# The first image's 5x5 convolution computed by pairs of rows with shared products

## The chip, the core and the metric

The kernel runs on one core of one Trainium2 chip. The metric is the device time in microseconds of one execution. A core has five engines that run side by side, each with its own queue of instructions in order: TensorE (PE, matrix products into PSUM), VectorE (DVE), ScalarE (ACT), GpSimd (POOL) and SyncE (SP, which here issues DMA transfers). They wait for each other by semaphores.

## What is computed

Four images of 128 channels and 64 x 64 pixels pass through four layers, each with a group normalisation ahead of it and the input added to its result. All data is float32. Cut to what matters:

```
x = x + attention(group_norm(x))        # layer 0, all 4096 pixels against all
x = x + conv5x5(group_norm(x), c)       # layer 1, 128 -> 128 channels, zero padding 2
x = x + selective_scan(group_norm(x))   # layer 2, a recurrence over the 4096 pixels
x = x + conv3x3(group_norm(x), main_w)  # layer 3, 128 -> 128 channels, zero padding 1
```

The 25 taps `c` of layer 1 are themselves built from tables (`weightsxx`, `weightsidentity`, picked by the radius of the tap), so they are computed on the chip at the start.

## The kernel before

Channels lie on the 128 partitions, pixels along the free dimension. The program is written as Python generators: `images()` strings together the work of the four images for everything except the recurrence, and `scan_core` is the recurrence itself, in ticks of 1024 pixels. Each `yield` hands back an estimate of the TensorE time just recorded (`PRODUCT`, 0.86 us for one 128x512 product). The loop at L1088 records one tick of the scan and then as much of `images()` as a credit (`pace`) allows, so the order of the instructions on every engine is written out by hand, and the work of images 1 to 3 is laid between the ticks of the scan of earlier images. Image 0 has no scan to lie beside: its attention is recorded first (L1060 to L1066, with the building of the 5x5 taps laid into its start), and then `before(0)` draws its convolution and the first part of its scan preparation before the first tick.

`conv` (L542) does a convolution. It clears the borders of a padded copy of the image, `xp` (L549 to L552, four memsets on GpSimd), normalises the image into it in four quarters on ScalarE (`piece`), and then, for each of 8 blocks of 8 rows (512 pixels), adds up k x k products in one PSUM bank:

```
nc.tensor.matmul(
    acc.rearrange("p (r w) -> p r w", w=W), weights[:, t, :],
    xp[:, y : y + RPM, dx : dx + W],
    start=t == 0, stop=t == k * k - 1 and not residual,
)
```

Each tap is one weight matrix of 128 x 128, and each product reads 8 rows of 64 pixels, shifted by the tap. Banks go round by the tags `s`, `a`, `z`. After the third product of the next block, `finish` takes the block away. For layer 1 this is `add` (L952): VectorE adds the bank to `xs`, the running image, and takes the statistics (`bn_stats`) for the next group norm. Then `scan_prep` (L590) normalises `xs` and goes on.

The names that matter below: `xs` the running image; `xp` (in traces `xpe` for layer 1, `xpm` for layer 3) the padded normalised image; `cw` the 25 taps; `m3` the 9 taps of layer 3, loaded at the start on ScalarE's queue (L111); `pce` the PSUM bank of a block; tags `A0`, `A1`, `V` and `xt` the large buffers of which each convolution takes one. `build_conv_weights` (L214) makes `cw` on VectorE. `L405`, `L411`, `L417` are the attention's scores, exponentials and values, `L459` its sums of exponentials, taken on VectorE and GpSimd for image 0. `L808` and `L839` are the GpSimd products of the scan, `L818` its recurrence on VectorE, and `br`, `cr` the rows that it loads through SyncE's queue (L784). The whole program is recorded twice; the second copy (`program(True)`), a safer form of the attention, runs only where a sum of exponentials has left its range.

Of the kernel before, what the change touches and what calls it, by code (L numbers as in the profile page):

```python
# [24 lines left out]
F32 = mybir.dt.float32  # L25
I32 = mybir.dt.int32
AF = mybir.ActivationFunctionType
ALU = mybir.AluOpType
# [4 lines left out]
P = 128  # L33
GROUPS = 32
GN_EPS = 1e-5
CH = 1024
MM = 512
HALF = P // 2
PAD = 2
# [6 lines left out]
PRODUCT, HOP, SLOT, PACE, ENDPACE, AHEAD = 0.86, 1.7, 0.7, 2.9, 1.5, 4  # L46
# [6 lines left out]
def conv_preact_kernel(  # L53
# [16 lines left out]
    nc = tc.nc  # L70
    B, C, H, W = x.shape
    L = H * W
# [4 lines left out]
    NTAP = xhat.shape[1]  # L77
    HP, WP = H + 2 * PAD, W + 2 * PAD
# [3 lines left out]
    RPM = MM // W  # L82
# [4 lines left out]
    const = ctx.enter_context(tc.tile_pool(name="const", bufs=1))  # L87
    small = ctx.enter_context(tc.tile_pool(name="small", bufs=2))
    dram = ctx.enter_context(tc.tile_pool(name="dram", bufs=2, space=DRAM))
    ps = ctx.enter_context(tc.tile_pool(name="ps", bufs=1, space=PSUM))  # L90
    pools, ready = {}, set()

    def bank(tag, name):
        return pools.get(tag, ps).tile([P, MM], F32, tag=tag, name=name)
# [12 lines left out]
    nc.scalar.dma_start(wback[:, 0, :], mats[:, 4, :])  # L107
    nc.scalar.dma_start(wback[:HALF, 1, :], mats[HALF:, 4, :])
    nc.scalar.dma_start(wback[HALF:, 1, :], mats[:HALF, 4, :])
    m3 = const.tile([P, main_w.shape[1], C], F32, name="m3")  # L110
    nc.scalar.dma_start(m3, main_w)  # L111

    ident = const.tile([P, P], F32, name="ident")
    make_identity(nc, ident)
# [18 lines left out]
    for d in range(2):  # L133
        r = slice(d * HALF, (d + 1) * HALF)
# [74 lines left out]
    nc.vector.tensor_scalar(hbias, cbias, 0.5, None, ALU.mult)  # L209


    cw = const.tile([P, NTAP, C], F32, name="cw")

    def build_conv_weights(tmp):  # L214
        xx_sb = tmp.tile([P, NTAP, C], F32, name="xx_sb")
        nc.sync.dma_start(xx_sb, xhat)
        id_sb = tmp.tile([P, C], F32, name="id_sb")
        nc.sync.dma_start(id_sb, identity)
        picked = tmp.tile([P, 2, NTAP, C // 2], F32, name="picked")
        for n, (which, table, inds) in enumerate((("xx", wxx, indsxx), ("id", wid, indsid))):  # L220
            nr, oc = table.shape[1], table.shape[2]
            acc = picked[:, n]
            one = cw.rearrange("p k c -> p (k c)")[:, : NTAP * oc]
            one = one.rearrange("p (k o) -> p k o", o=oc)
            tab = tmp.tile([P, nr, oc], F32, name=f"tab{which}")
            nc.sync.dma_start(tab, table)
            ii = tmp.tile([P, NTAP], I32, name=f"ii{which}")
            nc.sync.dma_start(ii, inds.to_broadcast([P, NTAP]))
            fi = tmp.tile([P, NTAP], F32, name=f"fi{which}")
            nc.vector.tensor_copy(fi, ii)  # L230

            ng = tmp.tile([P, NTAP], F32, name=f"ng{which}")
            nc.vector.tensor_scalar(ng, fi, 0.0, float(nr), ALU.is_lt, ALU.mult)
            nc.vector.tensor_tensor(fi, fi, ng, ALU.add)
            nc.vector.tensor_scalar(fi, fi, 0.0, float(nr - 1), ALU.max, ALU.min)
            for r in range(nr):
                hit = tmp.tile([P, NTAP], F32, name=f"hit{which}{r}")
                nc.vector.tensor_scalar(hit, fi, float(r), None, ALU.is_equal)
                hit_b = hit.unsqueeze(2).to_broadcast([P, NTAP, oc])
                tab_b = tab[:, r : r + 1, :].to_broadcast([P, NTAP, oc])  # L240
                if r == 0:
                    nc.vector.tensor_tensor(acc, tab_b, hit_b, ALU.mult)
                else:
                    nc.vector.tensor_tensor(one, tab_b, hit_b, ALU.mult)
                    nc.vector.tensor_tensor(acc, acc, one, ALU.add)
                yield HOP

        for t in range(2):
            def every(ap):
                return ap.rearrange("p k (o t) -> p k o t", t=2)[:, :, :, t]  # L250

            idb = id_sb.rearrange("p (o t) -> p o t", t=2)[:, :, t].unsqueeze(1)
            idb = idb.to_broadcast([P, NTAP, C // 2])
            nc.vector.tensor_tensor(every(xx_sb), every(xx_sb), picked[:, 0], ALU.mult)
            nc.vector.tensor_tensor(every(cw), picked[:, 1], idb, ALU.mult)
            yield HOP
        nc.vector.tensor_tensor(cw, cw, xx_sb, ALU.add)

    ASIZE, VSIZE = (H + 4) * (W + 4), (H + 2) * (W + 2)

    def large(n, name):
        return pools["big"].tile([P, ASIZE], F32, tag=f"A{n % 2}", name=name)
# [6 lines left out]
    def stats_tile(name):  # L272
        return small.tile([P, NM, 6], F32, tag=f"gn_st{name[0]}", name=f"st_{name}")
# [36 lines left out]
    def normalise(dst, src, gn):  # L310
        nc.scalar.activation(dst, src, AF.Identity, scale=gn[0], bias=gn[1])  # L311
# [230 lines left out]
    def conv(b, xs, tag, st, weights, k, finish, name, residual=False):  # L542

        pad = k // 2
        hp, wp = H + 2 * pad, W + 2 * pad
        size = VSIZE if tag == "V" else ASIZE
        xp = pools["big"].tile([P, size], F32, tag=tag, name=f"xp{name}_{b}")
        xp = xp[:, : hp * wp].rearrange("p (h w) -> p h w", w=wp)
        nc.gpsimd.memset(xp[:, :pad, :], 0.0)  # L549
        nc.gpsimd.memset(xp[:, hp - pad :, :], 0.0)  # L550
        nc.gpsimd.memset(xp[:, pad : hp - pad, :pad], 0.0)
        nc.gpsimd.memset(xp[:, pad : hp - pad, wp - pad :], 0.0)  # L552
        gn = yield from group_norm(st, f"{name}{b}")
        xh = xs.rearrange("p (h w) -> p h w", w=W)

        def piece(i):
            h0, h1 = i * H // 4, (i + 1) * H // 4
            normalise(xp[:, pad + h0 : pad + h1, pad : pad + W], xh[:, h0:h1, :], gn)

        piece(0)  # L560
        yield HOP / 2
        piece(1)
        done = None
        for i in range(NM):
            if i < 2:
                piece(2 + i)
            acc = bank("saz"[i % 3], f"pc{name}_{b}_{i}")
            for t in range(k * k):
                dy, dx = divmod(t, k)
                y = i * RPM + dy  # L570
                nc.tensor.matmul(  # L571
                    acc.rearrange("p (r w) -> p r w", w=W), weights[:, t, :],
                    xp[:, y : y + RPM, dx : dx + W],
                    start=t == 0, stop=t == k * k - 1 and not residual,
                )
                if t == 2 and done is not None:
                    finish(*done)
                if t % 3 == 2:
                    yield 3 * PRODUCT
            if residual:  # L580
                nc.tensor.matmul(acc, ident, xs[:, bass.ts(i, MM)], start=False, stop=True)
            yield PRODUCT
            done = i, acc
        yield HOP
        finish(*done)

# [334 lines left out]
    def program(safe):  # L923
        mats4, ynds, ends = {}, {}, {}
        ready.clear()

        def load(tile, b):
            for c in range(NCH):
                nc.sync.dma_start(tile[:, bass.ts(c, CH)], xf[b][:, bass.ts(c, CH)])
                yield 0.0  # L930
# [13 lines left out]
        def front(b, xn, v):  # L944

            xs = large(b + 1, f"xs_{b}")[:, :L]
            yield from load(xs, b)
            st = stats_tile(f"e{b}")
            yield from attention(b, xs, xn, v, st, safe)
            st2 = stats_tile(f"s{b}")  # L950

            def add(i, acc):  # L952
                cut = bass.ts(i, MM)
                nc.vector.tensor_tensor(xs[:, cut], acc, xs[:, cut], ALU.add)
                nc.vector.bn_stats(st2[:, i, :], xs[:, cut])

            yield from conv(b, xs, f"A{b % 2}", st, cw, 5, add, "e")

            def mat(name):
                return dram.tile([NCH, P, CH], F32, tag=name, name=f"{name}_{b}")  # L960

            mats4[b] = (
                [mat("bm"), mat("cm")], mat("dd"), mat("dxd"), mat("xcd"),
                dram.tile([P, L], F32, tag="xsd", bufs=B, name=f"xsd_{b}"),
            )
            ynds[b] = dram.tile([NM, P, MM], F32, tag="ynd", bufs=B, name=f"ynd_{b}")
            operands = yield from scan_prep(b, xs, st2, mats4[b])
            if b + 1 < B:
                return (yield from both(operands, start(b + 1, 10)))
            yield from operands  # L970
# [52 lines left out]
        inner, last = range(PER, NM - PER), range(NM - PER, NM)  # L1023
# [15 lines left out]
        with ExitStack() as es, tc.manual_schedule():  # L1039
# [60 lines left out]
            for _ in chain(end(B - 1, range(PER)), back(B - 1)):  # L1100
                pass

    program(False)


# [11 lines left out]
    with tc.If(again > 0):  # L1117
        program(True)
# [59 lines left out]
```

## Time and profile before

| | |
|---|---|
| time, median of 3 runs | 4684.2 us (4680.76 to 4685.26) |
| span of the profiled run | 4679.2 us, mean granted TensorE clock 0.941 |
| TensorE matmul | 4151.4 us busy (89%) |
| VectorE | 3764.6 us busy (80%) |
| GpSimd | 3522.0 us busy (75%) |
| ScalarE | 2313.3 us busy (49%) |
| HBM | 153 GB/s over the span |
| the convolution of image 0 (L571) | 542.3 to 717.5 us of the span, 400 records of 200 products |

Engines work side by side, so the busy times don't add up. The shares are means over stages that differ, and what an edit is worth has to be read in the stage in which it lies. A float32 product of 128x512 appears as two MATMUL records. A line such as `L571 PE MATMUL pce<-xpe,cw 128*128 128x512 f32 x400 | busy, mean ns | idle before, releaser` reads: source line, engine, operation, output and inputs, shape, count; time in which the group kept its engine busy, mean length of one; time for which the engine stood idle ahead of it, and what ended most of that.

### The profile page before, as it was taken

The page shows a single profiled execution, that of the slowest core. Times are in us where ns is not written, and L with a number is a line of the kernel's source. Part 1 is how long each engine was busy: PE and PEld are TensorE (multiplying, and loading weights), DVE is VectorE, ACT ScalarE, POOL GpSimd, SP SyncE. Part 2 cuts the span into 40 slices and gives each one's busy share as a digit, 9 for nine tenths or more (in the row PEclk, how much of TensorE's full clock was granted, in tenths as well). Part 3 has the DMA queues.
Part 4 walks back from the last instruction along what each step waited for, and adds up shares of the span by engine and source line. Part 5 has one row for each costly group of instructions (what it writes and reads, how often), then busy time and mean ns, then how long its engine had stood idle before and what let it go on. Part 6 is the DMA issues. An engine that isn't in the chain of part 4 may idle for free. (4 is left out here: it accounts for less than half of the span.)

```text
span 4679.2 us, 43928 instructions
## 1 busy us (share of the span) xinstructions
PE 4151.4 (89%) x13840; PEld 1538.3 (33%) x13840; DVE 3764.6 (80%) x3673; ACT 2313.3 (49%) x4166; POOL 3522.0 (75%) x1644
## 2 busy tenths in 40 slices
PE   6999997999999988999999979999999748576767
PEld 3444443333333323333333323333333202121212
DVE  7222104999999998999999999899989899999993
ACT  2333205666665356666654466666543644444431
POOL 2333202898888978898989869888889689999992
PEclk9999998999999999999999989999999968787878
DMA  1000005544444555445444564454445565656561
GB/s 65 0 0 1 0 5 184 186 168 163 163 169 150 178 203 214 155 164 175 169 158 164 187 227 169 157 177 164 168 147 177 201 224 199 229 193 229 186 230 46
DMA packets 210434, 718.90 MB, mean 154 GB/s; under 512 B 24848, under 2 KB 25744, under 8 KB 210064
## 3 DMA queue, kind: packets, MB, share of 16 engines
q1 hardware_dynamic: 208448, 714.69, 43.7%
q8 instruction: 111, 1.82, 0.2%
q10 hardware_dynamic: 1744, 1.32, 0.1%
q14 instruction: 131, 1.07, 0.1%
HBM read 649.07 MB, written 66.85 MB: 153 GB/s over the span
## 5 line engine op out<-in xcount | busy, mean ns | idle before, releaser
L808 POOL TENSOR_TENSOR db<-dx,br 128x1024 f32<-128x1024 f32 x1024 | 2404.4, 2367 | 377.8 <-DVE hc L818 94.8
L801 ACT ACTIVATE da<-de,a_neg 128x512 f32<-128x512 f32 (+1 forms) x1795 | 1343.9, 752 | 926.9 <-DVE da L818 600.3
L405 PE MATMUL sc<-r,x 128*128 128x512 f32 x2048 | 1087.5, 613 | 44.0 <-ACT last L834 16.4
L417 PE MATMUL acc<-pt,v 128*128 128x512 f32 x2048 | 1049.1, 594 | 1.5
L839 POOL TENSOR_TENSOR hc<-hc,cr 128x1024 f32<-128x1024 f32 x392 | 928.5, 2369 | 19.0 <-ACT last L834 15.5
L411 ACT ACTIVATE pt<-sc 128x512 f32<-128x512 f32 x1024 | 604.0, 590 | 613.4 <-PE sc L405 577.8
L821 DVE TENSOR_TENSOR hc<-da,cr 128x512 f32<-128x512 f32 (+1 forms) x1095 | 847.1, 774 | 71.7 <-DVE da L818 0.9
L853 PE MATMUL y<-hc,sel 128*32 128x512 f32 x4096 | 654.0, 653 | 272.7 <-POOL hc L839 247.5
L818 DVE TENSOR_TENSOR_SCAN da<-da,last,db 128x512 f32<-128x512 f32 (+1 forms) x474 | 740.5, 1562 | 16.2 <-POOL db L808 8.9
L571 PE MATMUL pce<-xpe,cw 128*128 128x512 f32 x1600 | 724.6, 606 | 24.8 <-ACT xpe L311 17.8
L818 DVE TENSOR_TENSOR_SCAN da<-da,da,db 128x512 f32<-128x512 f32 x463 | 595.8, 1287 | 26.2 <-ACT da L801 25.8
L405 PEld LDWEIGHTS sc<-r,x 128*128 128x128 f32 x2048 | 358.9, 190 | 642.7 <-issue 385.9
L417 PEld LDWEIGHTS acc<-pt,v 128*128 128x128 f32 x2048 | 388.4, 190 | 498.9 <-issue 480.0
L571 PEld LDWEIGHTS pce<-xpe,cw 128*128 128x128 f32 x1600 | 297.3, 190 | 452.4 <-issue 424.0
L818 DVE TENSOR_TENSOR_SCAN hc<-da,last,db 128x512 f32<-128x512 f32 (+1 forms) x294 | 442.7, 1506 | 2.9 <-POOL db L808 1.2
L818 DVE TENSOR_TENSOR_SCAN hc<-da,hc,db 128x512 f32<-128x512 f32 x308 | 395.1, 1283 | 45.1 <-ACT da L801 15.6
L459 POOL TENSOR_TENSOR sidep<-sidep,pt 128x512 f32<-128x512 f32 x120 | 161.3, 1344 | 307.0 <-ACT pt L411 307.0
L853 PEld LDWEIGHTS y<-hc,sel 128*32 128x32 f32 x4096 | 93.5, 111 | 728.7 <-POOL hc L839 333.2
L571 PE MATMUL pcm<-xpm,m 128*128 128x512 f32 x576 | 287.5, 647 | 31.4 <-ACT xpm L311 31.4
L459 DVE TENSOR_TENSOR sided<-sided,pt 128x512 f32<-128x512 f32 x120 | 90.3, 753 | 249.7 <-ACT pt L411 248.4
L818 DVE TENSOR_TENSOR_SCAN da<-da,db 128x512 f32<-128x512 f32 (+1 forms) x158 | 235.7, 1492 | 17.0 <-ACT da L801 9.3
L834 ACT COPY last<-da 128x1 f32<-128x1 f32 x473 | 74.0, 156 | 270.1 <-DVE hc L821 268.2
(167 smaller groups left out, 2251.9 us busy)
## 6 DMA issues: line engine op xcount, KB each, us to landing
br<-bm SPq DMA_DIRECT2D x512, 512.0 KB, 5.0
cr<-cm SPq DMA_DIRECT2D x512, 512.0 KB, 3.9
de<-dd SPq DMA_DIRECT2D x64, 512.0 KB, 4.6
dx<-dxd SPq DMA_DIRECT2D x64, 512.0 KB, 6.2
x<-in_x_dram SPq DMA_DIRECT2D x16, 512.0 KB, 5.7
xs<-in_x_dram SPq DMA_DIRECT2D x16, 512.0 KB, 6.8
xsd<-xs SPq DMA_DIRECT2D x16, 512.0 KB, 5.1
xcd<-xc SPq DMA_DIRECT2D x16, 512.0 KB, 2.7
```

The costliest lines, as they stand in the source:

```text
L405: nc.tensor.matmul(sc, xn[:, bass.ts(j, P)], rq[blk], start=True, stop=True)
L411: nc.scalar.activation(pt, sc, AF.Exp)
L417: nc.tensor.matmul(acc[blk], v[:, j, :], ring[:, u % NRING, :], start=j == 0, stop=j == NJT - 1)
L459: eng.tensor_tensor(s, s, ring[:, u % NRING, :], ALU.add)
L571: nc.tensor.matmul(acc.rearrange("p (r w) -> p r w", w=W), weights[:, t, :], xp[:, y : y + RPM, dx : dx + W], start=t == 0, stop=t == k * ...
L801: nc.scalar.activation(da, rep["de", b, c, d, g][:, bass.ts(h, size)], AF.Exp, scale=a_neg[:, at(i)])
L808: nc.gpsimd.tensor_tensor(dbs[i], rep["dx", b, c, d, g], rows["b", b, c, d, q], ALU.mult)
L818: nc.vector.tensor_tensor_scan(h, da, db[:, cut], before, ALU.mult, ALU.add)
L821: nc.vector.tensor_tensor(hc[:, cut], h, rows["c", b, c, d, q][:, cut], ALU.mult)
L834: nc.scalar.copy(last[b][:, at(i)], end)
L839: nc.gpsimd.tensor_tensor(hcs[i], hcs[i], rows["c", b, c, d, q], ALU.mult)
L853: nc.tensor.matmul(y[r : r + SG, :], sel, hcs[i - KG + 1 + gg][:, bass.ts(h, MM)], start=q == 0, stop=False, tile_position=(0, r), skip_gr ...
```

## The change

For image 0 alone the 5x5 convolution is computed two rows at a time. With w0 to w4 the five rows of taps (each five products wide) and x0 to x5 six rows of the padded image, two neighbouring rows of the result are

```
even = w0 x0 + w1 x1 + w2 x2 + w3 x3 + w4 x4
odd  = w0 x1 + w1 x2 + w2 x3 + w3 x4 + w4 x5
```

Both hold (w1 + w2) x2 + (w3 + w4) x4, if the rest is put into differences of rows:

```
q    = (w1 + w2) x2 + (w3 + w4) x4
even = q + w0 x0 + w1 (x1 - x2) + w3 (x3 - x4)
odd  = q + w0 x1 + w2 (x3 - x2) + w4 (x5 - x4)
```

So ten rows of products become eight: two shared, three for the even and three for the odd row. A product still has 512 columns, now 8 pairs' worth of even or of odd rows. The sums of taps are made once on VectorE. The differences of rows are made on GpSimd, into a buffer `diffs` with tag `V`. The shared part `q` leaves its bank through ScalarE (`qs`), and GpSimd adds it to both halves of `xs`; VectorE then adds the even and odd banks as `add` did before. Images 1 to 3 keep the plain convolution.

To make room, `cw` grows by ten matrices, and `m3` loses its own place: it shares that of the first nine taps, so it is loaded after the last 5x5 convolution, and a copy of the taps (`kept`) is put into DRAM for the safer copy of the program. The padded image keeps a border only on the left of each row: the border at the right is the left one of the next row, and a view shifted by the padding reads across. This goes for all convolutions.

```diff
-    m3 = const.tile([P, main_w.shape[1], C], F32, name="m3")
-    nc.scalar.dma_start(m3, main_w)
...
+    SUM12, SUM34 = 5, 6
+    cw = const.tile([P, NTAP + 10, C], F32, name="cw")
+    taps5 = cw[:, :NTAP, :]
+
+    m3 = cw[:, : main_w.shape[1], :]
+    kept = dram.tile([P, main_w.shape[1], C], F32, tag="kept", bufs=1, name="kept")
...
+        nc.vector.tensor_tensor(taps5, taps5, xx_sb, ALU.add)
+        for n in range(2):
+            row = cw[:, (1 + 2 * n) * 5 :]
+            nc.vector.tensor_tensor(
+                cw[:, NTAP + n * 5 : NTAP + (n + 1) * 5, :], row[:, :5], row[:, 5:10], ALU.add
+            )
+        nc.sync.dma_start(kept, m3)
...
     def conv(b, xs, tag, st, weights, k, finish, name, residual=False):
-        hp, wp = H + 2 * pad, W + 2 * pad
+        hp, wp = H + 2 * pad, W + pad
...
-                    xp[:, y : y + RPM, dx : dx + W],
+                    views[dx > pad][:, y : y + RPM, dx - (dx > pad) * pad :][:, :, :W],
...
+    def conv_pairs(b, xs, tag, st, st2, lean):
...
+        def odd(j, n):
+            nc.gpsimd.tensor_tensor(
+                diffs[:, j * WQ : (j + n) * WQ].rearrange("p (h w) -> p h w", w=WQ),
+                rows[:, 2 * j + 1 : 2 * (j + n) : 2, :], rows[:, 2 * j + 2 : 2 * (j + n) + 1 : 2, :],
+                ALU.subtract,
+            )
...
+        def add(c, y, acc):
+            nc.vector.tensor_tensor(chunk(xs, c, y), flat(acc), chunk(xs, c, y), ALU.add)
+            if y == 1:
+                for i in (2 * c, 2 * c + 1):
+                    nc.vector.bn_stats(st2[:, i, :], xs[:, bass.ts(i, MM)])
+
+        for c in range(L // CH):
+            j = c * CK
+            if c < 2:
+                piece(2 + c)
+            if c < 3:
+                differences(c + 1)
+            accs = [
+                (bank("s", f"pq_{b}_{c}"), ((SUM12, image, 2 * j + 2), (SUM34, image, 2 * j + 4))),
+                (bank("a", f"pe0_{b}_{c}"),
+                 ((0, image, 2 * j), (1, diff, j), (3, diff, j + 1))),
+                (bank("z", f"pe1_{b}_{c}"),
+                 ((0, image, 2 * j + 1), (2, diff, NP + j + 1), (4, diff, NP + j + 2))),
+            ]
...
+                if n == 0:
+                    qs = pools["bg"].tile([P, MM], F32, tag="w", bufs=4, name=f"q_{b}_{c}")
+
+                    def done(acc=acc, qs=qs, c=c):
+                        nc.scalar.copy(qs, acc)
+                        for y in range(0 if lean else 2):
+                            nc.gpsimd.tensor_tensor(
+                                chunk(xs, c, y), chunk(xs, c, y), flat(qs), ALU.add
+                            )
...
-            yield from conv(b, xs, f"A{b % 2}", st, cw, 5, add, "e")
+            if b == 0:
+                yield from conv_pairs(b, xs, f"A{b % 2}", st, st2, False)
+            else:
+                yield from conv(b, xs, f"A{b % 2}", st, cw, 5, add, "e")
+            if b + 1 == B:
+                nc.sync.dma_start(m3, main_w)
```

More of the change, by code (lines that the diff above doesn't have):

```diff
@@ L209, in conv_preact_kernel @@
     nc.vector.tensor_scalar(hbias, cbias, 0.5, None, ALU.mult)
-    cw = const.tile([P, NTAP, C], F32, name="cw")
+    SUM12, SUM34 = 5, 6
[3 more added lines that the diff above has]
+    kept = dram.tile([P, main_w.shape[1], C], F32, tag="kept", bufs=1, name="kept")
     def build_conv_weights(tmp):
@@ L249, in every @@
             def every(ap):
-                return ap.rearrange("p k (o t) -> p k o t", t=2)[:, :, :, t]
+                return ap.rearrange("p k (o t) -> p k o t", t=2)[:, :NTAP, :, t]
             idb = id_sb.rearrange("p (o t) -> p o t", t=2)[:, :, t].unsqueeze(1)
@@ L256, in build_conv_weights @@
             yield HOP
-        nc.vector.tensor_tensor(cw, cw, xx_sb, ALU.add)
-    ASIZE, VSIZE = (H + 4) * (W + 4), (H + 2) * (W + 2)
+        nc.vector.tensor_tensor(taps5, taps5, xx_sb, ALU.add)
[5 more added lines that the diff above has]
+        nc.sync.dma_start(kept, m3)
+    ASIZE, VSIZE = HP * (W + PAD) + PAD, (H + 2) * (W + 2) + PAD
     def large(n, name):
@@ L544, in conv @@
         pad = k // 2
-        hp, wp = H + 2 * pad, W + 2 * pad
+        hp, wp = H + 2 * pad, W + pad
         size = VSIZE if tag == "V" else ASIZE
         xp = pools["big"].tile([P, size], F32, tag=tag, name=f"xp{name}_{b}")
-        xp = xp[:, : hp * wp].rearrange("p (h w) -> p h w", w=wp)
+        nc.gpsimd.memset(xp[:, (hp - pad) * wp : hp * wp + pad], 0.0)
+        views = [
+            xp[:, o : o + hp * wp].rearrange("p (h w) -> p h w", w=wp) for o in (0, pad)
+        ]
+        xp = views[0]
         nc.gpsimd.memset(xp[:, :pad, :], 0.0)
-        nc.gpsimd.memset(xp[:, hp - pad :, :], 0.0)
         nc.gpsimd.memset(xp[:, pad : hp - pad, :pad], 0.0)
-        nc.gpsimd.memset(xp[:, pad : hp - pad, wp - pad :], 0.0)
         gn = yield from group_norm(st, f"{name}{b}")
@@ L585, in conv, with piece, even, differences @@
         finish(*done)
+    def conv_pairs(b, xs, tag, st, st2, lean):
+        NP, CK = H // 2, CH // W // 2
+        WQ = W + PAD
+        xp = large(b, f"xpe_{b}")
+        rows = xp[:, : HP * WQ].rearrange("p (h w) -> p h w", w=WQ)
+        xh = xs.rearrange("p (h w) -> p h w", w=W)
+        nc.gpsimd.memset(rows[:, :PAD, :], 0.0)
+        nc.gpsimd.memset(xp[:, (HP - PAD) * WQ : HP * WQ + PAD], 0.0)
+        nc.gpsimd.memset(rows[:, PAD : HP - PAD, :PAD], 0.0)
+        gn = yield from group_norm(st, f"e{b}")
+        diffs = pools["big"].tile([P, VSIZE], F32, tag="V", name=f"df_{b}")
+        nc.gpsimd.memset(diffs[:, 2 * (NP + 1) * WQ :], 0.0)
+        def piece(i):
+            h0, h1 = i * H // 4, (i + 1) * H // 4
+            normalise(rows[:, PAD + h0 : PAD + h1, PAD:], xh[:, h0:h1, :], gn)
+        def odd(j, n):
[4 more added lines that the diff above has]
+            )
+        def even(j, n):
+            at = (NP + j) * WQ
+            nc.gpsimd.tensor_tensor(
+                diffs[:, at : at + n * WQ].rearrange("p (h w) -> p h w", w=WQ),
+                rows[:, 2 * j + 1 : 2 * (j + n) : 2, :], rows[:, 2 * j : 2 * (j + n) - 1 : 2, :],
+                ALU.subtract,
+            )
+        def differences(i):
+            last = i == 3
+            odd(8 * i, 8 + last)
+            even(8 * i + 1, 8 + last)
+        def by_rows(t, n):
+            return [t[:, o : o + n * WQ].rearrange("p (h w) -> p h w", w=WQ) for o in (0, PAD)]
+        padded, differ = by_rows(xp, HP), by_rows(diffs, 2 * (NP + 1))
+        def image(r, dx):
+            late = dx // PAD > 0
+            dx -= late * PAD
+            return padded[late][:, r : r + 2 * CK - 1 : 2, dx : dx + W]
+        def diff(r, dx):
+            late = dx // PAD > 0
+            dx -= late * PAD
+            return differ[late][:, r : r + CK, dx : dx + W]
+        def chunk(t, c, y):
+            v = t[:, bass.ts(c, CH)].rearrange("p (h t w) -> p h t w", t=2, w=W)
+            return v[:, :, y, :]
+        def flat(t):
+            return t.rearrange("p (h w) -> p h w", w=W)
+        piece(0)
+        yield HOP / 2
+        piece(1)
+        differences(0)
+        K5 = 5
+        steps, done = [], None
+        def add(c, y, acc):
[15 more added lines that the diff above has]
+                 ((0, image, 2 * j + 1), (2, diff, NP + j + 1), (4, diff, NP + j + 2))),
+            ]
+            for n, (acc, parts) in enumerate(accs):
+                k, total = 0, len(parts) * K5
+                for w, view, r in parts:
+                    for dx in range(K5):
+                        k += 1
+                        nc.tensor.matmul(
+                            flat(acc), cw[:, w * K5 + dx, :], view(r, dx),
+                            start=k == 1, stop=k == total and (n == 0 or not lean),
+                        )
+                        if k == 3 and done is not None:
+                            done()
+                            done = None
+                        if k % 3 == 0:
+                            yield 3 * PRODUCT
+                if n == 0:
[3 more added lines that the diff above has]
+                        for y in range(0 if lean else 2):
+                            nc.gpsimd.tensor_tensor(
+                                chunk(xs, c, y), chunk(xs, c, y), flat(qs), ALU.add
+                            )
+                    yield PRODUCT
+                else:
+                    if lean:
+                        nc.tensor.matmul(acc, ident, qs, start=False, stop=True)
+                        yield PRODUCT
+                    def done(acc=acc, c=c, y=n - 1):
+                        add(c, y, acc)
+        yield HOP
+        done()
@@ L925, in program @@
         ready.clear()
+        if safe:
+            nc.sync.dma_start(m3, kept)
         def load(tile, b):
@@ L955, in add @@
                 nc.vector.bn_stats(st2[:, i, :], xs[:, cut])
-            yield from conv(b, xs, f"A{b % 2}", st, cw, 5, add, "e")
+            if b == 0:
+                yield from conv_pairs(b, xs, f"A{b % 2}", st, st2, False)
+            else:
+                yield from conv(b, xs, f"A{b % 2}", st, cw, 5, add, "e")
+            if b + 1 == B:
+                nc.sync.dma_start(m3, main_w)
             def mat(name):
```

## The prediction

> **What bounds the kernel now.** I read the page's slices first, to see in which stage the edited work lies, then the windows around that stage, then the groups of instructions inside it, and last the timeline at its two ends.
>
> The slices are 117 us each:
>
> ```profile
> PE   6999997999999988999999979999999748576767
> DVE  7222104999999998999999999899989899999993
> ACT  2333205666665356666654466666543644444431
> POOL 2333202898888978898989869888889689999992
> ```
>
> Slices 1 to 5 have TensorE alone at 9 with every other engine at 0 to 3: image 0 runs its attention and its 5x5 convolution by itself, before the scan begins in slice 6. From there on VectorE and GpSimd are both at 8 to 9, and images 1 to 3 run their attention and convolutions beside the scan. The edited convolution is the last part of the lonely stage. The windows show it (columns: stretch, length, then busy time and count of TensorE, its weight loads, VectorE, ScalarE and GpSimd, granted clock, DMA share, GB/s):
>
> ```profile
> 500.00:600.00 100.00, 92.37 (x228) 41.97 (x227) 13.64 (x28) 15.97 (x23) 13.33 (x18) 0.95 0.01 6
> 600.00:650.00 50.00, 50.00 (x117) 21.80 (x116) 2.77 (x4) 0.00 (x0) 0.00 (x0) 1.00 0.00 0
> 650.00:700.00 50.00, 50.00 (x117) 21.72 (x116) 4.16 (x6) 0.00 (x0) 0.00 (x0) 1.00 0.00 0
> ```
>
> From 600 to 700 us TensorE is busy for all of it, GpSimd and ScalarE for none. The groups from 542 to 717.5 us say what ends whose wait:
>
> ```profile
> L571 PE MATMUL pce<-xpe,cw 128*128 128x512 f32 x400 | 175.1, 599 | 7.1 <-ACT xpe L311 7.1
> L954 DVE TENSOR_TENSOR xs<-pce,xs 128x512 f32<-128x512 f32 x7 | 4.8, 691 | 147.3 <-PE pce L571 147.3
> L955 DVE BATCH_NORM_STATS2 st_s<-xs 128x6 f32<-128x512 f32 x7 | 4.9, 694 | 0.2
> ```
>
> 200 matmuls (two records each, since the data is f32) keep TensorE busy for 175.1 us without a wait inside, and VectorE waits 147.3 us for it. Every microsecond taken from these products is a microsecond less before the scan starts. The two ends, from the timeline:
>
> ```profile
> 542.35 39.83 PE L571 MATMUL pce<-xpe,cw 128*128 128x512 f32 x87 [7.07 <-ACT xpe L311]
> ...
> 717.51 0.69 DVE L954 TENSOR_TENSOR xs<-pce,xs 128x512 f32<-128x512 f32 x1 [20.12 <-PE pce L571]
> ...
> 718.23 0.69 DVE L955 BATCH_NORM_STATS2 st_s<-xs 128x6 f32<-128x512 f32 x1
> ...
> 722.45 4.63 ACT L311 ACTIVATE xn<-xs,nb_s,rs_s 128x1024 f32<-128x1024 f32 x4 [176.76 <-POOL nb_s L306]
> ```
>
> The reader is to see that after the last product only a short chain (one addition, one statistics instruction, the group norm) stands between the convolution and the next stage.
>
> **What the Trainium skill says.** GPSIMD Engine Reference, section 3.1 (Elementwise): a two-input f32 operation on GpSimd costs about twice VectorE's, 4497 ns for 2048 elements per partition. The trace agrees: L808 takes 2367 ns for 1024, L459 takes 1.26 us for 512 where nothing disturbs it. SBUF — State Buffer, section "Who interferes with whom": GpSimd and VectorE share ports only when VectorE has two SBUF inputs, and TensorE and ScalarE never wait. In this stage VectorE's additions have one input in PSUM, so I add nothing for contention; no row here shows that case. TensorE: Matmul & The Clock Gate, "What's actually happening": after an idle spell the array runs at half clock for some 3.4 us. The trace agrees: the granted clock is 0.50 from 540 to 545 us and 0.87 to 550. This start is in both kernels.
>
> **The change part by part.**
>
> 1. Products of image 0. Before: 8 blocks of 25 taps, 200 matmuls. After: 4 chunks of 16 rows, each with 10 shared products, and 15 for the even and 15 for the odd rows: 160. Once the clock is full, the weight loads follow each other every 0.4326 us (19 steps from 708.23 to 716.45 us), so one f32 matmul takes 0.865 us; 40 fewer take off 34.6 us. The shape stays 128x512. The access differs: shared products and the direct ones read every second row (528 bytes apart instead of 272). I take the same rate, because this kernel's matmuls run at one rate whatever they read: 595 ns a record for rows of 68 (5x5), 592 for rows of 66 (3x3), and the L631 taps, half of which read a reversed view, also start 0.43 us apart.
>
> 2. Differences on GpSimd: 8 subtractions over 8 or 9 rows of 66 (528 to 594 elements), by L459 about 1.3 to 1.5 us each, 11 us in all, where GpSimd is idle. The first four must be there for chunk 0: they can start when the first quarter is normalised (542.3) and are done by about 548. The first product that reads a difference is the 16th. At half clock for the first three and 0.865 us after that it comes at about 557. Nine microseconds of slack, so even a duration twice as long would not show. Later differences are a chunk (34 us) ahead.
>
> 3. The shared sum: 4 ScalarE copies (0.6 us, row L411's size) and 8 GpSimd additions into xs (1.3 us each, 11 us in all). The VectorE addition that needs them comes 15 products (13 us) after the copy; copy and two additions take 3.3 us. The bank of the shared product is wanted again only at the next chunk, 30 products on. Hidden under TensorE.
>
> 4. VectorE at the end of the convolution: still 8 additions and 8 statistics, but a chunk's two statistics now both come after its last addition. At the end, that is one more L955 on the path: +0.7 us.
>
> 5. Sums of neighbouring tap rows when the weights are built: two VectorE additions over 640 elements. L257 adds 3200 in 3.48 us, so 0.70 us each, 1.4 us together. Here VectorE is the bound:
>
> ```profile
> 90.00:100.00 10.00, 7.23 (x17) 2.83 (x16) 9.66 (x7) 2.77 (x5) 4.60 (x2) 1.00 0.00 0
> ```
>
> TensorE is at 7.2 of 10 because side sums queue on VectorE behind the weights, and the exponentials wait for ring slots. So I charge all of it: +1.4 us. The copy of the first taps to DRAM queues on SyncE with nothing behind it until after the convolution: nothing.
>
> 6. The 3x3 weights no longer load at the start (576 KB) but into the 5x5 taps' place once image 3's convolution ends. At the start, x's load begins after the small weight products (15.17 us), which queue on VectorE behind the rates' load. That load is issued 0.6 us earlier, but two small VectorE operations now stand behind it, 0.4 us. I take zero, at most 1 us either way. Late: the load waits on SyncE for the last 5x5 product, and the next row load (br) queues behind it. In the trace of before that br is issued at 3647.77 and the last product ends about 3651.3, so it moves 4 us, and some 4 us of shared transfer more. Its data is first wanted by a GpSimd product at 3667.78, and it lands after 4.7 us: still hidden. First use of the 3x3 weights is near 3861: hidden.
>
> 7. Padding of all other convolutions: rows of 66 and 65 instead of 68 and 66, and one memset fewer (0.15 to 0.26 us of GpSimd) per convolution, seven times: at most 1.5 us, most of it while GpSimd waits anyhow. I take nothing.
>
> The order in which the instructions of images 1 to 3 and the scan stand is otherwise the same, so from the scan on the program is shifted. Sum: -34.6 + 0.7 + 1.4 = -32.5 us, 4684.2 - 32.5 = 4651.7 us.
>
> **The rivals.**
>
> A. Part of the gain is given back: TensorE waits for differences or shared sums (GpSimd on strided rows could be slower than any row here), or the late load of weights and the shifted scan cost a few microseconds. If strided GpSimd operations took three times L459 (4 us), the four first differences end at 558.5 instead of 548, some 1.5 us too late once; a stall of the scan by the late load, if br were not hidden, is its 8 us. Together: about 4661 us. For it: the scan stage has waits in all directions, and no row shows GpSimd on such views. Against: the slack above.
>
> B. Reading every second row slows TensorE. 80 of the 160 products do so; at 1.5 times the duration, +34.6 us and the gain is gone: about 4686 us, no change. Against: the equal rates of three kinds of view.
>
> C. The new rows slow the other convolutions. 600 matmuls of 5x5 and 288 of 3x3 remain; 5% on each is 888 x 0.043 = 38 us, if all of it is on the path: 4651.7 + 38 = 4690 us, no better than before; with a loss beside it, slower. For it: in these stages TensorE is at 9 too. Against: 66 and 68 wide rows already take 592 and 595 ns.
>
> **How the numbers follow.** Forecast 0.80, A 0.12, B 0.04, C 0.04. The predicted time is 4652 us. Downwards I leave room for the memsets, the start and the 2 to 4 us by which three runs differ: 4643. Upwards the range takes in A: 4664. Faster by over 0.2% means below 4674.8 us: the forecast and A give 0.92, from which I keep 0.01 for worse forms of A: 0.91. B is mostly within 0.2%, C is split: same 0.05, slower 0.04.
>
> **What would show it.** In the changed kernel's profile the products of image 0 should be 320 records over about 141 us, starting near 543 us with no wait for GpSimd inside; GpSimd some 22 us busy there with operations of 1.3 to 1.5 us; the group norm after it some 33 us earlier than 718; and the distance from there to the end unchanged within 5 us. A record of these products well above 600 ns would mean B, the same in the later convolutions C, idle time before products that read the differences A. The prediction is wrong if the stage shrinks but the end does not move with it.

## The result and the profile after

The changed kernel takes 4653.6 us (median of 4 runs, 4652.7 to 4654.1) against 4684.05 us: a ratio of 0.9936 with a 95% interval of 0.9919 to 0.9953, 30.4 us less. The forecast was 4652 us, the range 4643 to 4664.

The slices of the changed kernel (116 us each) look like those of before. In slice 6 (counted from 0), VectorE and GpSimd are now at 6 and 4 instead of 4 and 2, because the scan starts earlier in it:

```profile
PE   6999998999999979999999979999999748576767
...
DVE  7222116899999998999999998999999899999993
...
POOL 2333204889888968898988868898889689999992
```

The groups of instructions in image 0's convolution, 544 to 690 us (busy, mean ns of one, idle before):

```profile
L698 PE MATMUL pe<-df,cw 128*128 128x512 f32 x160 | 70.0, 592 | 0.0
L698 PE MATMUL pq<-xpe,cw 128*128 128x512 f32 x80 | 37.2, 621 | 7.1 <-ACT xpe L321 7.1
L698 PE MATMUL pe<-xpe,cw 128*128 128x512 f32 x80 | 35.9, 594 | 0.0
L713 POOL TENSOR_TENSOR xs<-xs,q 128x512 f32<-128x512 f32 x8 | 10.0, 1268 | 98.6 <-ACT q L711 98.6
...
L632 POOL TENSOR_TENSOR df<-xpe 128x528 f32<-128x528 f32 (+1 forms) x4 | 4.6, 1152 | 0.0
L624 POOL TENSOR_TENSOR df<-xpe 128x528 f32<-128x528 f32 (+1 forms) x4 | 4.5, 1132 | 1.3 <-ACT xpe L321 1.3
```

320 records instead of 400, and no product waits for a difference: the idle column of the reads of `df` is 0.0. Reading every second row (`pe<-xpe`) takes 594 ns a record, reading whole rows of the differences 592. The 621 of the shared products (`pq`) holds the start at half clock; the 62 of them that come after 555.2 us take 594. GpSimd needs 19.1 us for all its new work, while it would be idle.

The end of the stage, from the timeline (start, length, idle before):

```profile
676.17 8.75 PE L698 MATMUL pe<-df,cw 128*128 128x512 f32 x20
685.03 0.69 DVE L675 TENSOR_TENSOR xs<-pe,xs 128x512 f32<-128x512 f32 x1 [12.23 <-PE pe L698]
...
685.75 1.29 DVE L678 BATCH_NORM_STATS2 st_s<-xs 128x6 f32<-128x512 f32 x2
...
690.50 4.64 ACT L321 ACTIVATE xn<-xs,nb_s,rs_s 128x1024 f32<-128x1024 f32 x4 [30.79 <-POOL nb_s L316]
```

The next stage's normalisation starts at 690.50 instead of 722.45 us, 31.95 us earlier. From first product to last the convolution takes 140.1 us instead of 175.1. Its start, however, is at 544.86 instead of 542.35 us, so 2.5 us were lost before it. Where, the windows at the start show (columns as in the prediction; the last is cut to the stretch of lower clock):

```profile
90.00:100.00 10.00, 7.16 (x13) 2.62 (x12) 9.65 (x9) 2.17 (x4) 4.23 (x2) 0.84 0.14 59
98.19:101.60 3.41, 3.21 (x4) 1.52 (x5) 3.10 (x4) 1.23 (x3) 1.39 (x1) 0.50 0.00 0
```

The granted clock from 90 to 100 us is 0.84; before it was 1.00. Part of the 0.84 is older than the sums: up to 91.4 us TensorE still runs at half clock after an earlier wait, which differs from run to run. The other part is the 3.41 us from 98.19. The timeline of TensorE there names the cause:

```profile
94.53 1.02 PE L427 MATMUL acc<-pt,v 128*128 128x512 f32 x2
98.39 2.08 PE L415 MATMUL sc<-r,x 128*128 128x512 f32 x2 [2.84 <-ACT pt L421]
100.26 1.70 PE L427 MATMUL acc<-pt,v 128*128 128x512 f32 x2
```

The kernel before, at the same score product:

```profile
97.45 1.13 PE L405 MATMUL sc<-r,x 128*128 128x512 f32 x2 [1.37 <-ACT pt L411]
98.42 1.02 PE L417 MATMUL acc<-pt,v 128*128 128x512 f32 x2
```

TensorE waits 2.84 us instead of 1.37 for the exponentials, which wait for VectorE. After the longer wait a product takes 2.08 us instead of 1.13. VectorE itself shows what the sums cost: in the changed kernel

```profile
94.54 2.51 DVE L264 TENSOR_TENSOR cw<-cw 128x640 f32<-128x640 f32 x2
96.97 5.53 DVE L469 TENSOR_TENSOR sided<-sided,pt 128x512 f32<-128x512 f32 x6
```

and before

```profile
94.96 6.61 DVE L459 TENSOR_TENSOR sided<-sided,pt 128x512 f32<-128x512 f32 x6
```

2.51 + 5.53 - 6.61 = 1.43 us more on VectorE. The exponential that follows comes 1.47 us later than in the kernel before, relative to those ahead of the sums. A few exponentials on, it is 3.05 us: the other 1.6 us are TensorE's, at the lower clock. Since the exponential ahead of the sums came 0.5 us earlier than before (91.20 instead of 91.73 us), 2.5 us are left at the convolution's start.

After image 0 the shift only drifts: the start of the scan's GpSimd products is 32.2 us earlier in image 0's scan, 31.4 in image 1's, 31.0 in image 2's and 28.7 in image 3's; the profiled spans differ by 27.5 us. The medians differ by 30.4. From image 0's normalisation to the end it is 3961.2 us in the changed kernel and 3956.7 in the kernel before, but 3969.6 in a second profile of the kernel before, which alone took between 4679.6 and 4696.7 us beside the experiments. For a drift of 4.5 us in one pair of profiles no cause can be shown.

### The profile page after: what moved, and what is told of

Its sections match the earlier page's. It is cut to its first block, busy times and chain, and to the rows that moved or that the text cites. A ratio compares the mean times of both kernels' runs of the same rounds, so it can differ in the third digit from the quotient of the medians.

```text
span 4651.7 us, 43791 instructions
## 1 busy us (share of the span) xinstructions
PE 4124.6 (89%) x13760; PEld 1527.9 (33%) x13760; DVE 3765.8 (81%) x3675; ACT 2316.4 (50%) x4170; POOL 3537.1 (76%) x1653
## 3 DMA queue, kind: packets, MB, share of 16 engines
q14 instruction: 133, 1.08, 0.1%
## 5 line engine op out<-in xcount | busy, mean ns | idle before, releaser
L583 PE MATMUL pce<-xpe,cw 128*128 128x512 f32 x1200 | 547.7, 607 | 17.5 <-ACT xpe L321 10.4
L427 PEld LDWEIGHTS acc<-pt,v 128*128 128x128 f32 x2048 | 388.9, 191 | 499.9 <-issue 481.0
L583 PEld LDWEIGHTS pce<-xpe,cw 128*128 128x128 f32 x1200 | 222.2, 191 | 344.5 <-issue 323.3
L583 PE MATMUL pcm<-xpm,cw 128*128 128x512 f32 x576 | 292.0, 655 | 30.8 <-ACT xpm L321 30.8
```

The lines of the kernel that those rows point to most:

```text
L427: nc.tensor.matmul(acc[blk], v[:, j, :], ring[:, u % NRING, :], start=j == 0, stop=j == NJT - 1)
L583: nc.tensor.matmul(acc.rearrange("p (r w) -> p r w", w=W), weights[:, t, :], views[dx > pad][:, y : y + RPM, dx - (dx > pad) * pad :][:, : ...
```

## The experiments

Times are medians; ratios are against the kernel before, run beside them on the same chip.

**All of the change except the pairs.** One line is different from the changed kernel:

```diff
-            if b == 0:
+            if b < 0:
                 yield from conv_pairs(b, xs, f"A{b % 2}", st, st2, False)
```

> All of the change except the pairs: image 0 goes back to 200 plain products; the new rows, the sums of taps and the late load of the 3x3 weights stay. Theory (the gain is the 40 products, the rest costs what the start showed): the products take 175 us again (400 records), image 0's convolution begins 2.5 us later than before, and the end comes 1 to 3 us later than before, 4685 to 4688 us. Rival (part of the gain came from the new rows, the shorter memsets or the moved weights): it ends below 4682 us.

Measured: 4687.9 us (12 runs), ratio 1.0002 (0.9994 to 1.0011). The products are back at 175 us:

```profile
L583 PE MATMUL pce<-xpe,cw 128*128 128x512 f32 x400 | 174.4, 599 | 7.1 <-ACT xpe L321 7.1
```

They begin at 544.92 us, as in the changed kernel. So the gain at the end is that of the pairs; what the new rows, the sums, the fewer memsets and the moved 3x3 weights do together lies between 3 us less and 5 us more by the interval. Within the stage the new rows take 0.7 us off (174.4 instead of 175.1), and the pairs 34.3 (174.4 less 140.1).

**The sums of taps later.**

```diff
         nc.vector.tensor_tensor(taps5, taps5, xx_sb, ALU.add)
+        for _ in range(24):
+            yield HOP
         for n in range(2):
```

> The two sums of taps are recorded 24 steps of the attention later, where VectorE has idle time. Theory (they cost 3.0 us because they stand in VectorE's backlog, and TensorE's idle time there also lowers its clock): image 0's convolution begins about 3 us earlier than in the changed kernel, at about 540.5 us instead of 543.6, and the end comes 2 to 4 us earlier, about 4650.5 us. Rival (the delay comes from elsewhere, such as the copy of the taps to DRAM or the earlier start): it begins within 0.5 us of the changed kernel's, and the end is the same, 4653.6 us.

Measured: 4648.75 us (4646.3 to 4650.6, 4 runs), ratio 0.9920 (0.9903 to 0.9936). Image 0's convolution begins at 542.4 us; the expectation's 543.6 and 540.5 are those of the normalisation ahead of it, which now is at 541.1. The two sums, now at 127.7 us, take 1.48 and 0.81 us, and nobody waits for them. The window at the old place:

```profile
90.00:100.00 10.00, 8.54 (x20) 3.34 (x19) 9.58 (x8) 3.02 (x6) 4.60 (x2) 1.00 0.14 59
```

The clock is full there, 1.00 instead of 0.84. The columns at the end (DMA share 0.14, 59 GB/s) are those of the changed kernel: the copy of the taps to DRAM did not move with the sums, it is issued at 94.41 us here and at 94.53 in the changed kernel. So the copy, which the rival names, is not the cause. The medians differ by 4.9 us, more than the 2.5 us at this place; the intervals of the two ratios touch, and the rest is within the scatter of the scan stages.

**The shared sum through TensorE** (`conv_pairs` has this as `lean`).

```diff
-                yield from conv_pairs(b, xs, f"A{b % 2}", st, st2, False)
+                yield from conv_pairs(b, xs, f"A{b % 2}", st, st2, True)
```

> The shared sum is added by TensorE: one more product with the identity per even and odd bank, 8 in all, and no GpSimd additions into the image. Theory (GpSimd's 8 additions are hidden, TensorE is the bound of the stage): the stage grows by 8 x 0.865 = 6.9 us, the end by about 7 us. Rival (GpSimd's additions or VectorE's wait for them cost something): it grows by clearly less than 6 us.

Measured: 4660.9 us in one run. From first product to last the convolution takes 147.45 us instead of 140.06:

```profile
L719 PE MATMUL pe<-q,ident 128*128 128x512 f32 x16 | 8.2, 592 | 0.0
```

7.4 us more for 8 products, and nothing won by taking GpSimd out. GpSimd's additions are hidden.

**Each difference twice.**

```diff
-            odd(8 * i, 8 + last)
-            even(8 * i + 1, 8 + last)
+            for _ in range(2):
+                odd(8 * i, 8 + last)
+                even(8 * i + 1, 8 + last)
```

> Each difference of rows is computed twice on GpSimd, which adds 8 operations of about 1.1 us. Theory (nine microseconds of slack ahead of the first reader, a chunk for the others): the products still take 140 us without idle time inside, and image 0's next group norm comes at the same time within 0.3 us. Rival (the differences sit on the path): TensorE idles before the products that read them, 2 us or more.

Measured: 4648.45 us in one run. GpSimd's share doubles, the products don't wait:

```profile
L632 POOL TENSOR_TENSOR df<-xpe 128x528 f32<-128x528 f32 (+1 forms) x8 | 9.2, 1154 | 0.0
L624 POOL TENSOR_TENSOR df<-xpe 128x528 f32<-128x528 f32 (+1 forms) x8 | 9.1, 1132 | 1.3 <-ACT xpe L321 1.3
```

The convolution takes 139.98 us against 140.06, and from its start to the next normalisation it is 145.56 us against 145.64. This single run is 5 us shorter than the changed kernel's median, for which no cause is shown; the runs of the kernel before beside it spread over 12 us.

**Pairs in all four images,** first with shared sums through GpSimd, then with the identity in images 1 to 3.

```diff
-            if b == 0:
-                yield from conv_pairs(b, xs, f"A{b % 2}", st, st2, False)
+            if b >= 0:
+                yield from conv_pairs(b, xs, f"A{b % 2}", st, st2, b > 0)
```

The first of the two has `False` in the place of `b > 0`.

> Pairs of rows for all four images, shared sums through GpSimd. Images 1 to 3 each save 40 products (34.6 us of TensorE) and add about 19 us to GpSimd, beside the scan. Theory 1 (there the scan on VectorE and GpSimd sets the pace, and the extra work stands in its way): no gain, 0 to 60 us slower than the changed kernel, 4654 to 4714 us. Theory 2 (TensorE's work beside the scan sets the end, since what is not done by the end of an image's scan is done alone after it): up to 3 x 34.6 us faster, down to about 4555 us.

> Pairs of rows for all four images; in images 1 to 3 the shared sum is added by TensorE with the identity, so that each saves 32 products (27.7 us of TensorE) and adds only the differences, about 9 us, to GpSimd. Theory 1 (scan bound): 0 to 30 us slower than the changed kernel, 4654 to 4684 us, and less slow than with shared sums through GpSimd. Theory 2 (TensorE bound): up to 3 x 27.7 us faster, down to about 4570 us.

Measured: 4661.1 us, ratio 0.9953 (0.9935 to 0.9970), and 4647.5 us, ratio 0.9922 (0.9906 to 0.9939). TensorE has about 100 and 80 us less to do than in the changed kernel, and the end hardly moves: the first lies in the range of theory 1, the second 6.5 us below it and far above that of theory 2. In the second kernel image 3's scan preparation starts at 3530.9 instead of 3632.1 us, but its scan at 3722.8 instead of 3708.8. The work ends early and the scan doesn't. This looked like a scan set by VectorE and GpSimd alone. The lower pace below shows that it is not.

**The same with late sums, then with a lower pace.** The pace is the TensorE time recorded beside each tick of the scan.

```diff
-PRODUCT, HOP, SLOT, PACE, ENDPACE, AHEAD = 0.86, 1.7, 0.7, 2.9, 1.5, 4
+PRODUCT, HOP, SLOT, PACE, ENDPACE, AHEAD = 0.86, 1.7, 0.7, 2.7, 1.5, 4
```

> Pairs in all four images (shared sum by the identity in images 1 to 3) and the late sums of taps together. Theory (the two act in different stages, the second before the scan, the first hardly at all because the scan sets the pace): about 3 us below the kernel with the late sums alone at the most, 4643 to 4649 us. Rival (the products saved beside the scan are worth their time after all): well below 4640 us.

> The same with the pace of TensorE's work per tick of the scan lowered from 2.9 to 2.7 us, so that the smaller work of images 1 to 3 is spread over the whole scan instead of ending some 110 us early. Theory (VectorE and GpSimd set the length of a tick whatever TensorE has beside them): within 6 us of the same kernel at the old pace. Rival (a tick is long because TensorE's work stands in it, so that less work per tick shortens it): 20 us or more faster, up to 7% of the three scans beside other images.

Measured: 4646.5 us at pace 2.9 (ratio 0.9910, 0.9896 to 0.9925), 4627.3 us at 2.7 (0.9872, 0.9856 to 0.9888). The first is where the theory had it. At the second the theory fell: the kernel is 19 us faster, not within 6 (the rival had 20 or more), so less TensorE work per tick did shorten the ticks.

**A control, a step between, and the other form.** The control has pairs in image 0 only, late sums and pace 2.8. The second has the identity form in images 1 to 3 at 2.8. The third has shared sums through GpSimd in all images at 2.7.

> Control for the pace: pairs in image 0 only, sums late, pace 2.8 instead of 2.9. Theory (TensorE stands in every tick, so that a lower pace shortens ticks but leaves more of the plain convolutions' work to be done alone at the end of an image's scan): no gain to speak of, within 5 us of the 4648.8 us at pace 2.9. Rival (2.9 was simply too high, for any kernel): 8 us or more faster, 4640 us or less.

> Pairs in all images (identity in images 1 to 3), sums late, pace 2.8. Theory: between the 4646.5 us at pace 2.9 and the 4627.3 us at 2.7, about 4637 us, since half of the freed TensorE time is spread. Rival (a step, not a slope): at one of the two ends within 3 us.

> As the kernel with pace 2.7, but the shared sums of images 1 to 3 go through GpSimd: 8 products fewer (6.9 us of TensorE) and 8 additions on GpSimd more (about 10 us) per image. Theory (GpSimd is as full as TensorE beside the scan): slower by 5 to 30 us, as at pace 2.9 where the difference was 13.5 us. Rival (TensorE alone is the bound there): faster, up to 20 us.

| pairs in | shared sums, images 1 to 3 | pace 2.9 | pace 2.8 | pace 2.7 |
|---|---|---|---|---|
| image 0 | - | 4648.8 | 4675.7 | - |
| all | identity | 4646.5 | 4615.2 | 4627.3 |
| all | GpSimd | 4661.1 (sums early) | - | 4607.6 |

Ratios of the three new ones: 0.9974 (0.9966 to 0.9982), 0.9844 (0.9826 to 0.9862) and 0.9830 (0.9812 to 0.9847). In none of the three did the theory hold. The control is not equal but 27 us slower at the lower pace, which its rival did not have either; the second is neither a slope nor a step; in the third the rival held: GpSimd's form is faster than the identity's at 2.7, by 19.7 us.

The scans themselves say why. Each image's scan starts 256 products on GpSimd (`db<-dx,br`). The table has the time from the first start to the 231st and from there to the last, summed over the scans of images 0 to 2, from one profile each, all with late sums:

| pairs in, pace | first 230 steps | last 25 steps |
|---|---|---|
| image 0, 2.9 | 2565.6 us | 367.2 us |
| image 0, 2.8 | 2551.8 us | 422.6 us |
| all (identity), 2.9 | 2595.7 us | 363.9 us |
| all (identity), 2.8 | 2532.9 us | 380.8 us |
| all (identity), 2.7 | 2498.6 us | 419.9 us |
| all (GpSimd), 2.7 | 2516.0 us | 389.7 us |

Each step down in pace shortens the first part (by 14, 63 and 34 us), so there TensorE's work does hold the scan up, and lengthens the second (by 55, 17 and 39 us). What is left of the next image's work is done there, because `before` draws it ahead of that image's own scan: in image 0's scan of the control one step alone takes 53.8 us, at pace 2.9 none above 17.6. The medians move the way the sum of both parts does. GpSimd's form at 2.7 loses 17 us in the first part and wins 30 in the second; that its gain is near the 3 x 8 x 0.865 = 20.8 us of products that it saves is not shown to be more than chance.

Two windows show the same. From 1000 to 1400 us, in the middle of a scan, where GpSimd does nothing but the scan, the changed kernel, and its last 100 us of image 0's scan:

```profile
1000.00:1400.00 400.00, 393.58 (x1493) 144.48 (x1492) 370.06 (x376) 246.52 (x507) 359.02 (x155) 1.00 0.49 166
1625.00:1725.00 100.00, 81.41 (x294) 25.62 (x292) 91.19 (x115) 63.95 (x100) 68.58 (x35) 0.93 0.59 211
```

the control, likewise:

```profile
1000.00:1400.00 400.00, 390.64 (x1482) 142.08 (x1475) 374.34 (x381) 246.67 (x506) 361.78 (x157) 1.00 0.48 166
1640.00:1740.00 100.00, 83.49 (x275) 27.74 (x273) 71.07 (x98) 56.34 (x88) 49.44 (x28) 0.93 0.51 181
```

and the kernel with GpSimd's form at 2.7:

```profile
1000.00:1400.00 400.00, 389.50 (x1478) 140.81 (x1478) 379.15 (x387) 248.02 (x509) 369.17 (x160) 1.00 0.49 172
1620.00:1720.00 100.00, 80.78 (x281) 26.39 (x279) 81.76 (x106) 61.65 (x96) 59.67 (x32) 0.92 0.56 200
```

In the middle TensorE is busy 97 to 98% of the time in all three, and GpSimd gets through 155, 157 and 160 operations. At the end VectorE is at 91% in the changed kernel, 71% in the control and 82% in the last. A lower pace pays only if there is less to do, and pairs in all images make it less. Not tried: the best pace for each form, and the pace of the last image.

**The kernel before once more,** for a second profile of its start, without an edit.

> The kernel before once more, for a second profile of its start. Theory (the sums of taps explain the later start of image 0's convolution): from the first exponential of image 0 to the normalisation ahead of its convolution it is 499 us within 1 us again, against about 502 in the kernels with the sums in the backlog. Rival (TensorE's clock there varies by itself from run to run as much as that): 501 us or more.

Measured: 500.9 us from the first exponential to the normalisation, 499.1 in the first profile, so it lies between theory and rival. The six kernels with the sums in the backlog have 499.9 to 504.4, mean 502.1; the six with late sums and the two of before 498.6 to 500.9, mean 499.5. The ranges touch, because this stretch takes in other waits of TensorE, ahead of the sums and after them, that differ from run to run.

A shorter stretch sizes the term: from the exponential at about 91 us, just ahead of the sums, to the fortieth after it. It takes 73.35 or 73.36 us in all eight kernels without the sums there, both profiles of before among them; 76.25 to 76.52 us in five of the six with them; and 74.83 us in the sixth, the one with pairs in all images by the identity at pace 2.9. In all six TensorE's wait is 2.84 or 2.85 us. In the five the clock falls afterwards, in the sixth it does not:

```profile
98.31 1.13 PE L415 MATMUL sc<-r,x 128*128 128x512 f32 x2 [2.84 <-ACT pt L421]
99.27 1.02 PE L427 MATMUL acc<-pt,v 128*128 128x512 f32 x2
```

So the sums cost 1.47 us by VectorE wherever they stand in the backlog, and the lower clock 1.4 to 1.7 us more where it follows. For this stretch the rival is ruled out.

## Why the prediction was right

1. Products: 34.6 us forecast, 35.0 measured (175.1 less 140.1), of which 34.3 are the pairs' and 0.7 the new rows'. A record takes 592 to 595 ns, whatever rows are read; rival B is ruled out.
2. Differences on GpSimd: forecast at 1.3 to 1.5 us each, measured 1.13 and 1.15. The first four are done at 549.2 us and first read at 559.8, 10.6 us of slack where nine were forecast. Nothing waits, not even when each is done twice.
3. Shared sum: hidden as forecast. Taken off GpSimd, the stage only grows.
4. The extra statistics at the end: +0.7 us forecast. The distance from VectorE's last addition to its last group-norm transpose is 4.28 us instead of 3.76, +0.5.
5. Sums of taps: the one term that was mis-sized, 1.4 us against 3.05 here. VectorE's part was right, 1.47 us, though not in its pieces: the two sums take 2.51 us and the side sums behind them 1.08 less (the last section says why). Left out was TensorE's clock. The prediction used the Trainium skill's page "TensorE: Matmul & The Clock Gate", section "What's actually happening", for the start of the convolution only. That section speaks of an idle window of some 3.4 us that is not reset when a kernel starts; here a wait of 2.84 us, shorter than that, was followed by products of twice the length in five kernels of six. The measurement decides.
6. Weights of layer 3: nothing, as forecast, but one step was wrong. I had the late load wait on SyncE for the last 5x5 product. It overwrites only the first nine taps, and it was issued right after a `cr` row, at 3618.91 us, while the last product started at 3620.9 (columns: start, length):

```profile
3618.35 0.51 SPq L924 DMA_DIRECT2D cr<-cm  x1
3618.91 0.58 SPq L1104 DMA_DIRECT2D cw<-in_main_w_dram  x1
3619.55 0.52 SPq L924 DMA_DIRECT2D br<-bm  x1
```

The `br` row behind it moved 0.6 us, not 4. At the start the moved load brought the image's load 0.7 us forward (14.43 instead of 15.17 us), within the 1 us allowed; 0.5 us of it is left at the exponential ahead of the sums.
7. The other convolutions: the median record of the 5x5 products of images 1 to 3 takes 592 ns instead of 595, that of the 3x3 products 592 in both kernels. Rival C is ruled out.

The sum was -32.5 us, measured -30.4. Up to the next stage's normalisation it is -31.95 in the profile: -35.1 for the products, +0.5 for the statistics, +3.05 for the sums and their clock, -0.5 for the earlier start, -32.0 together. The mechanism was right, and this is where it was tested. The rest is the drift of the scan stages, whose scatter is larger than the miss: two profiles of the kernel before differ by 13 us behind this point. That the end came within 2 us of the forecast is therefore luck in part. Rival A in its stated form (waits for differences, a stall by the late load) did not happen.

## What to carry to other kernels

Fewer products pay one for one where TensorE works alone, and other engines' idle time there is a free place for the additions that save them. Where an order written by hand lays that engine's work beside another stage, saved work shows only after the order's own rate is set anew: here pairs in all images brought 2 us at the old pace and 60 us at a pace 0.1 us lower, while that pace alone cost 27 us. Small additions belong where their engine has no backlog, since a short extra wait of TensorE can cost as much again in clock (1.47 us of waiting here, 1.4 to 1.7 us of clock in five kernels of six).

## What the runs showed of the hardware that was not expected

**The same wait, with and without its price in clock.** In the changed kernel the stretch of half clock is 98.19 to 101.60 us, 3.41 us long. In the sixth kernel above the clock comes back to full at 89.62 us; counted on from there in steps of 3.41 us, one step ends inside the wait and so cuts it in two. The step ahead of the fall in the changed kernel, and the two steps that share the same wait in the sixth:

```profile
94.78:98.19 3.41, 0.77 (x2) 0.00 (x0) 3.31 (x4) 0.45 (x1) 0.85 (x1) 1.00 0.42 173
93.04:96.45 3.41, 2.42 (x6) 0.76 (x4) 3.38 (x3) 0.00 (x0) 2.50 (x1) 1.00 0.36 150
96.45:99.86 3.41, 1.55 (x4) 0.83 (x5) 3.10 (x5) 1.48 (x3) 0.97 (x1) 1.00 0.06 23
```

TensorE is busy 0.77 us of 3.41 in the first, 2.42 and 1.55 in the others; in the other four kernels whose clock fell, 0.91 to 1.39 us in the step ahead. All six fit a clock that goes by the work done in fixed steps, not by the length of one wait. That is read from traces; no experiment moved the wait against the steps.

**One collision that whichever operation stands there pays.** Two operations with both inputs in SBUF disturb each other on VectorE and GpSimd: while VectorE ran `cw<-cw,xx_sb`, GpSimd's 128x512 side sum took 3.20 us instead of 1.26, and the VectorE operation next in line was held up in turn. In the changed kernel that is the first sum of taps, 1.77 us where the second took 0.81; in the kernel before it is a side sum, 1.75 instead of 0.69. Since the collision is in both kernels it cancels, and so the prediction's 1.4 us for VectorE came out without it. This agrees with the Trainium skill, "SBUF — State Buffer", section "Who interferes with whom", which the prediction had set aside for the convolution, whose additions read PSUM, and had not applied to the building of the taps. The prediction's "only when VectorE has two SBUF inputs" is too narrow: the section names VectorE's 2-port modes as well, which no run here shows.
